# Last block of keys in a fused attention and expert kernel: three score products one place earlier, and the old maximum's weight sums added on GpSimd

## The chip, the core and the metric

The kernel runs on one core of a Trainium2 chip. A core has five engines that run side by side, each through its own queue in order: TensorE (PE: matrix products, with a separate queue for loading weights, PEld), VectorE (DVE), ScalarE (ACT), GpSimd (POOL) and SyncE (SP, which here issues all transfers). [...] The metric is the device time of one execution in microseconds (us); less is better.

## What is computed

One block of a network, in float32, on 128 rows `x` of width 512 and a context of 12544 rows: a cross-attention to the context (257 image rows, then text rows, each with its own softmax), a self-attention, and a routed mixture of experts. Only the cross-attention is touched:

```python
q = rms_norm(linear(x, q_w, q_b), norm_q_w)          # 16 heads of 32
k = rms_norm(linear(ctx_txt, k_w, k_b), norm_k_w)
v = linear(ctx_txt, v_w, v_b)
scores = einsum('bqhd,bkhd->bhqk', q, k) / sqrt(32)
probs  = softmax(scores)
txt_x  = einsum('bhqk,bkhd->bqhd', probs, v)
...
x = x + linear(txt_x + img_x, o_w, o_b)
```

## The kernel before, in words

**Tiling.** The text keys come in 24 blocks of 512 (the last has 511), block numbers 1 to 24; each block is cut into four tiles of 128 keys. Keys and values of a block are made by seven products of half-size blocks each (a Strassen scheme): `step(b, k, "k")` and `step(b, k, "v")` (line 1134) each issue one such product for block `b` and the VectorE or ScalarE instruction that takes it out of PSUM. The main loop (`for t in range(tile0[2], tile0[LAST])`) works on tile `t` and makes the next block's keys and values in between. What follows it is written out by hand for the last block, and this is where most of the change is.

**One tile.** For a tile, `weights(t)` (line 1249) first calls `scores(t)` (line 1162): 16 small products on PE into the one PSUM tile `sb` (four banks, one buffer). Then VectorE scales, subtracts the maximum and writes `p` (line 1258), and ScalarE takes the exponential in place (line 1266). `weigh` (line 1269) multiplies `p` by the values on PE (`av_new`). The softmax's denominator is gathered on GpSimd: `into_sums` (line 1427, instruction on line 1436) adds `p` into `ls`, and `half_into_sums` (line 1438, instruction on line 1440) does it in two halves of 1024 columns. `add_up` (line 1284) sums over the 128 keys of a tile on PE, into the PSUM bank `lpt`. `key_norms(b, js)` (line 1010) gives two tiles' norms: eight tiny PE products per tile pair (`ssq`), one or two VectorE instructions (`ms`), and GpSimd powers into `rinv`, which line 1258 reads. It needs `add_squares` (line 1126, two GpSimd additions on line 1130) to be done.

**Buffers.** `p` of most tiles lives in a pool of two buffers (`two`, tag `p`) that are handed out in turn; every third tile of the loop, and the first tile of the last block (`p_last`), has a buffer of its own. Call the last two tiles of block 23 Y and Z, and the four tiles of block 24 A, B, C and D (`t`, `t + 1`, `t + 2`, `t + 3`; D has 127 keys). Y and Z have the pool's two buffers, A has `p_last`, B gets Y's buffer, C gets Z's, D gets B's. A buffer is free when all readers of the tile before are done.

**Order.** Every instruction here goes through `pin` (line 838), so each engine's queue has the order of the program text. The queues of the stretch after the loop, before the change: PE: scores Z, keys step 7, norms A and B, scores A, weigh Y, weigh Z, keys step 4, values step 7, scores B, weigh A, values step 4, norms C and D, scores C, `lpt<-kept_l`, weigh B, add up B, scores D, weigh C, add up C, add up `ls`, add up D, weigh D. GpSimd: half sum Y, norms A and B, half sum Y, half sum Z, squares, half sum Z, norms C and D, sum A. After that come the reciprocals of `lpt`, the product with `w_o_w`, and the self-attention. `early_loads(0)` to `early_loads(2)` (line 1489) issue the next stage's weights into buffers as they come free.

**The old maximum.** The weights of the text tiles before tile `SWITCH` (the third of block 3) were taken against a first estimate of the maximum. From `SWITCH` on the kernel uses a better one; what was gathered before is multiplied by `shrink`. For the sums this is `kept_l`, made once at `SWITCH + 2` (line 1621, VectorE, from the PSUM bank `l_old`). In the kernel before it enters `lpt` by one product with the identity, on line 1684 in the last block.

Of the kernel before, what the change touches and what calls it, by code (L numbers as in the profile page):

```python
# [11 lines left out]
ALU = mybir.AluOpType  # L12
# [3 lines left out]
P = 128  # L16
# [4 lines left out]
XH, XHD = 16, 32  # L21
# [749 lines left out]
def fast_block(ctx: ExitStack, tc: tile.TileContext, a: dict, out: bass.AP, amiss: bass.AP):  # L771
    nc = tc.nc
# [11 lines left out]
    ident = const.tile([P, P], FP, tag="ident", name="ident")  # L784
# [53 lines left out]
    def pin(ins):  # L838

        return tc.keep_in_program_order(ins)  # L840
# [55 lines left out]
    with ExitStack() as xs:  # L896
# [113 lines left out]
        def key_norms(b, js):  # L1010

            ts = [blocks[b][3][j] for j in js]
            sp = bank(f"ssq_{b}_{js[0]}")
            for j, (o, m) in enumerate(ts):

                for r in range(0, m, XHD):
                    r1 = min(r + XHD, m)
                    pin(nc.tensor.matmul(  # L1018
                        sp[r:r1, j : j + 1],
                        lhsT=sq[b][:, 0, o + r : o + r1],  # L1020
                        rhs=ones[:, 0:1],
                        start=True,
                        stop=True,
                        skip_group_check=True,
                    ))
            ms = small.tile([P, 4], FP, tag="ms", name=f"ms_{b}_{js[0]}")
            t0 = tile0[b] + js[0]
            for j0, j1, m in row_groups(ts):
                pin(nc.vector.tensor_scalar(
                    ms[:m, j0:j1], sp[:m, j0:j1], 1.0 / D, 1e-6, ALU.mult, ALU.add  # L1030
                ))
                pin(inv_sqrt(rinv[:m, t0 + j0 : t0 + j1], ms[:m, j0:j1]))
# [101 lines left out]
        def step(b, k, kinds="kv"):  # L1134

            for kind in kinds:
                if k == 1:
                    if kind == "k":
                        kraw[b] = two.tile([P, NC, CHUNK], FP, tag="kraw", name=f"kraw_{b}")
                    else:  # L1140
                        vv[b] = two.tile([P, NC, D], FP, tag="v", name=f"v_{b}")
                    pin(nc.scalar.copy(piece(kind, "p1"), product(kind, b, 1, True)))  # L1142
                elif k == 2:
                    finish_quarter(kind, b, 0, 0, product(kind, b, 2, False), None)
                elif k == 6:
                    t = product(kind, b, 6, True)
                    pin(nc.vector.tensor_tensor(piece(kind, "z"), t, part_of[kind, "p1"], ALU.add))  # L1147
                elif k == 5:
                    t = product(kind, b, 5, True)
                    pin(nc.vector.tensor_tensor(piece(kind, "w"), t, part_of[kind, "z"], ALU.add))  # L1150
                elif k == 3:
                    finish_quarter(kind, b, 0, 1, product(kind, b, 3, False), part_of[kind, "z"])
                elif k == 7:
                    finish_quarter(kind, b, 1, 1, product(kind, b, 7, True), part_of[kind, "w"])
                elif k == 4:
                    finish_quarter(kind, b, 1, 0, product(kind, b, 4, False), part_of[kind, "z"])
                if kind == "k" and k in (3, 4):
                    squares(b, int(k == 4))
# [90 lines left out]
        def weights(t, s=None, p=None, parts=1):  # L1249

            b, part, o, m = tiles[t]
            if s is None:
                s = scores(t, "b")
            if p is None:
                p = two.tile([P, 4, CHUNK], FP, tag="p", name=f"p_{t}")
            n = 4 // parts
            for k in range(0, 4, n):
                pin(nc.vector.scalar_tensor_tensor(  # L1258
                    p[:m, k : k + n],
                    s[:m, k : k + n],  # L1260
                    rinv[:m, t : t + 1],
                    m_bc[part][:m, k : k + n],
                    ALU.mult,
                    ALU.subtract,
                ))
                pin(nc.scalar.activation(p[:m, k : k + n], p[:m, k : k + n], AF.Exp))  # L1266
            return p, s

        def weigh(t, p, first, last):

            b, part, o, m = tiles[t]
            for g in range(NC):
                for i in range(4):
                    hd = 4 * g + i
                    pin(nc.tensor.matmul(  # L1275
                        avp[part][i * XHD : (i + 1) * XHD, g, :],
                        lhsT=vv[b][:m, t - tile0[b], hd * XHD : (hd + 1) * XHD],
                        rhs=p[:m, i, g * P : (g + 1) * P],
                        start=(first and g == 0),
                        stop=(last and g == NC - 1),  # L1280
                        skip_group_check=True,
                    ))
# [64 lines left out]
        ps = [xc.tile([P, 4, CHUNK], FP, tag="ls", name="p_0")]  # L1347
# [61 lines left out]
        lp = bank("l_img")  # L1409
# [12 lines left out]
        SWITCH = tile0[RENEWED + 1] + 2  # L1422
        lsum = xc.tile([P, 4, CHUNK], FP, tag="ls", name="ls")
# [3 lines left out]
        def into_sums(t, p):  # L1427
            m = tiles[t][3]
            dst = [lsum[:m]] if t >= SWITCH else [h[:m] for h in ls_old]
            for k, d in enumerate(dst):  # L1430
                n = 4 // len(dst)
                src = p[:m, k * n : (k + 1) * n]
                if t in (t1, SWITCH):
                    pin(nc.gpsimd.tensor_copy(d, src))
                else:
                    pin(nc.gpsimd.tensor_tensor(d, d, src, op=ALU.add))  # L1436

        def half_into_sums(p, h):
            k = slice(2 * h, 2 * h + 2)
            pin(nc.gpsimd.tensor_tensor(lsum[:, k], lsum[:, k], p[:, k], op=ALU.add))  # L1440
# [100 lines left out]
        waiting = [pend]  # L1541
        AHEAD = range(NB - 8, NB - 2)
        for t in range(tile0[2], tile0[LAST]):
# [53 lines left out]
            if t == tile0[RENEWED + 1]:  # L1597
                m_new = xc.tile([P, 4, CHUNK], FP, tag="mx", name="mb_new")
                on_all(q_new, m_new, "new")
                pin(nc.vector.tensor_tensor(over, q_new, q_old, ALU.subtract))  # L1600
                less = small.tile([P, XH], FP, tag="less", name="less")
                pin(nc.scalar.activation(less, over, AF.Exp, scale=-1.0))
            elif t == tile0[RENEWED + 1] + 1:

                shrink = rowp.tile([P, D], FP, tag="h", name="shrink")
                on_heads(less, shrink, "less")
            elif t == SWITCH:
                av_old = avp["txt"].rearrange("p g q -> p (g q)")
                kept = {"av": row("kept_av", "kept_av")}
                pin(nc.vector.tensor_tensor(kept["av"], av_old, shrink, ALU.mult))  # L1610
                avp["txt"] = ps_o.tile([P, NC, P], FP, tag="o", name="av_new")
            elif t == SWITCH + 2:
                lp = bank("l_old")
                for i in range(4):
                    r = slice(i * XHD, (i + 1) * XHD)
                    pin(nc.tensor.matmul(
                        lp[r, :], lhsT=ones[:, :XHD], rhs=ls_old[i // 2][:, i % 2, :],
                        start=True, stop=True, skip_group_check=True,
                    ))
                kept["l"] = row("kept_l", "kept_l")  # L1620
                pin(nc.vector.tensor_tensor(kept["l"], lp, shrink, ALU.mult))
            if j == 2:
                make(b + 1, 3, "k")
            if b <= RENEWED:
# [38 lines left out]

        half_into_sums(unsummed[1], 0)
        step(b, 7, "k")
        key_norms(b, [0, 1])
        ps = [weights(t, p=xc.tile([P, 4, CHUNK], FP, tag="vw", name="p_last"))[0]]
        half_into_sums(unsummed[1], 1)
        for k_, p_ in waiting:
            weigh(k_, p_, False, False)  # L1670
        half_into_sums(p, 0)
        step(b, 4, "k")
        add_squares(b, 1)
        half_into_sums(p, 1)
        early_loads(0)
        step(b, 7, "v")
        ps.append(weights(t + 1)[0])
        weigh(t, ps[0], False, False)
        step(b, 4, "v")
        key_norms(b, [2, 3])  # L1680
        early_loads(1)
        ps.append(weights(t + 2)[0])
        lpt = bank("lpt")
        pin(nc.tensor.matmul(lpt, lhsT=ident, rhs=kept["l"], start=True, stop=False, skip_group_check=True))
        into_sums(t, ps[0])
        early_loads(2)
        weigh(t + 1, ps[1], False, False)
        add_up(lpt, ps[1], P, False, False)
        ps.append(weights(t + 3, parts=2)[0])
        weigh(t + 2, ps[2], False, False)  # L1690
        add_up(lpt, ps[2], P, False, False)
        add_up(lpt, lsum, P, False, False)
# [855 lines left out]
```

## Time and profile before

| what | value |
|---|---|
| device time, median of 3 runs | 1068.5 us (1067.93 to 1068.62) |
| device time of the profiled execution | 1066.76 us |
| its span (first to last instruction) | 1064.9 us, so 1.86 us lie around it |
| PE busy | 1047.9 us (98% of the span) |
| PEld, DVE, ACT, POOL busy | 829.6, 538.2, 360.1, 694.2 us |
| mean granted TensorE clock | 0.999 |
| stretch of the last block, 833 to 863 us: PE, PEld, DVE, ACT, POOL busy | 27.51, 19.35, 20.18, 12.52, 20.31 of 30 us |
| main loop, one block of four tiles | 33.5 us (from one block's first keys step to the next) |

How to read the views. In a timeline a line gives the start, the time from the first start to the last end, engine, source line, operation, output and inputs, shape and count; in brackets stands how long the engine had been idle, and whose end released it. Ends of PE products are modelled and overlap the next start, so for PE I take start to start. In the prediction all times are microseconds from the span's start.

### The profile page before, as it was taken

To read this page: it belongs to the slowest core of one execution; us is meant where nothing else is said; L and a number is where in the kernel's file an instruction comes from. 1 tells how busy PE (TensorE), PEld (TensorE's weight loads), DVE (VectorE), ACT (ScalarE), POOL (GpSimd) and SP (SyncE) were. 2 spreads that over 40 slices of the span, in tenths; PEclk is the share of its full clock that TensorE was granted. 3 is DMA by queue.
4 is the path that set the end of the run, shared out by engine and by line. 5 is a ranking of instruction groups with operands and counts; after the bars stand their busy time and mean duration, and the time that the engine had idled before them with its cause. 6 is when DMAs were issued, how large, how long until landed. Compare 5 with 4: busy or idle time off the path is not lost.

```text
span 1064.9 us, 24839 instructions
## 1 busy us (share of the span) xinstructions
PE 1047.9 (98%) x11076; PEld 829.6 (78%) x11076; DVE 538.2 (51%) x671; ACT 360.1 (34%) x438; POOL 694.2 (65%) x378
## 2 busy tenths in 40 slices
PE   9999999999999999999999999999999989999997
PEld 6768888888888888888888888888888769754332
DVE  2767764574445544455544555455444668442211
ACT  2353233333333333433334333343333424403111
POOL 2256888688888888888988889988999810000000
PEclk9999999999999999999999999999999999999999
DMA  9321021101111011110113301110010599629996
GB/s 298 108 81 37 6 81 50 41 2 41 41 41 41 2 41 41 42 39 3 42 45 116 101 14 41 41 41 15 27 41 2 172 353 389 224 72 412 415 413 241
DMA packets 43252, 113.25 MB, mean 106 GB/s; under 512 B 6720, under 2 KB 12032, under 8 KB 42112
## 3 DMA queue, kind: packets, MB, share of 16 engines
q1 hardware_dynamic: 43136, 111.57, 29.0%
q8 instruction: 89, 1.46, 0.6%
q14 instruction: 27, 0.22, 0.1%
HBM read 111.26 MB, written 0.29 MB: 105 GB/s over the span
## 4 chain that ended last, share of the span: by engine, by line
PE 94%; DVE 3%; ACT 1%; DMA 1%; POOL 1%; issue 0%; SPq 0%; DVEq 0%; ACTq 0%; POOLq 0%
PE kp L1085 28%; PE vp L1085 27%; PE sb L1169 10%; PE av_new L1275 7%; PE up L2135 5%; PE acc L2122 2%; PE qp L1794 1%; PE kp L1794 1%; PE yp L1952 1%; PE svp L1815 1%; PE y L2176 1%; PE vp L1237 1%; PE av_old L1275 1%; PE ssq L1018 1%; DVE p L1258 1%; DMA x<-in_x 1%
## 5 line engine op out<-in xcount | busy, mean ns | idle before, releaser
L1436 POOL TENSOR_TENSOR ls<-ls,p 128x2048 f32<-128x2048 f32 x79 | 359.7, 4553 | 31.0 <-ACT p L1266 31.0
L1266 ACT ACTIVATE p<-p 128x2048 f32<-128x2048 f32 (+1 forms) x95 | 179.9, 1893 | 437.3 <-DVE p L1258 425.7
L1258 DVE SCALAR_TENSOR_TENSOR p<-sb,rinv,mb_new 128x2048 f32<-128x2048 f32 (+1 forms) x86 | 199.9, 2325 | 108.8 <-PE sb L1169 107.1
L1130 POOL TENSOR_TENSOR sq<-sq 128x512 f32<-128x512 f32 x96 | 96.3, 1003 | 86.1 <-ACT sq L1124 82.3
L1169 PEld LDWEIGHTS sb<-qT_txt,kraw 32*128 32x128 f32 (+1 forms) x3040 | 93.4, 186 | 32.3 <-issue 30.7
L1169 PE MATMUL sb<-qT_txt,kraw 32*128 32x128 f32 (+1 forms) x3040 | 111.5, 283 | 0.4 <-DVE p L1258 0.4
L1085 PE MATMUL kp<-xs,w_k_w 128*128 128x256 f32 x384 | 95.4, 391 | 0.0
L1085 PE MATMUL kp<-ctx,w_k_w 128*128 128x256 f32 x384 | 93.2, 386 | 1.0 <-ACT kp L1142 1.0
L1085 PE MATMUL kp<-xs,kt 128*128 128x256 f32 x384 | 91.2, 380 | 0.1
L1085 PE MATMUL vp<-vt,xs 128*128 128x256 f32 x384 | 91.0, 380 | 0.0
L1085 PE MATMUL vp<-w_v_w,ctx 128*128 128x256 f32 x384 | 90.9, 380 | 0.0
L1085 PE MATMUL vp<-w_v_w,xs 128*128 128x256 f32 x384 | 90.8, 379 | 0.0
L1275 PE MATMUL av_new<-p,v 128*32 128x128 f32 (+1 forms) x2720 | 84.6, 274 | 0.5 <-ACT p L1266 0.5
L1085 PEld LDWEIGHTS kp<-xs,kt 128*128 128x128 f32 x384 | 72.5, 190 | 11.2 <-issue 0.9
L1085 PEld LDWEIGHTS vp<-vt,xs 128*128 128x128 f32 x384 | 72.7, 190 | 10.2 <-ACT kraw L1113 0.4
L1085 PEld LDWEIGHTS vp<-w_v_w,xs 128*128 128x128 f32 x384 | 72.8, 190 | 10.1
L1085 PEld LDWEIGHTS vp<-w_v_w,ctx 128*128 128x128 f32 x384 | 72.8, 190 | 10.0 <-issue 0.2
L1085 PEld LDWEIGHTS kp<-xs,w_k_w 128*128 128x128 f32 x384 | 69.2, 189 | 14.6 <-issue 4.8
L1085 PEld LDWEIGHTS kp<-ctx,w_k_w 128*128 128x128 f32 x384 | 70.8, 190 | 11.5 <-ACT kp L1142 1.4
L1275 PEld LDWEIGHTS av_new<-p,v 128*32 128x32 f32 (+1 forms) x2720 | 71.8, 110 | 7.1 <-ACT p L1266 1.4
L1147 DVE TENSOR_TENSOR kz<-kp,kp 128x512 f32<-128x512 f32 x24 | 16.6, 691 | 98.5 <-issue 93.9
L818 POOL TENSOR_TENSOR rs_x<-ve_x,neghalf 128x1 f32<-128x1 f32 x3 | 1.7, 552 | 95.5 <-DVE ve_x L826 95.5
(460 smaller groups left out, 1476.8 us busy)
## 6 DMA issues: line engine op xcount, KB each, us to landing
ctx<-in_ctxT SPq DMA_DIRECT2D x23, 1024.0 KB, 5.1
wo<-in_experts SPq DMA_DIRECT2D x18, 512.0 KB, 8.6
wo<-in_wo_codes SPq DMA_DIRECT2D x8, 512.0 KB, 6.3
wq<-in_experts SPq DMA_DIRECT2D x8, 512.0 KB, 9.8
wk<-in_experts SPq DMA_DIRECT2D x8, 512.0 KB, 9.5
wv<-in_experts SPq DMA_DIRECT2D x7, 512.0 KB, 10.0
q<-in_experts SPq DMA_DIRECT2D x7, 512.0 KB, 10.1
f<-in_experts SPq DMA_DIRECT2D x7, 512.0 KB, 10.0
```

The lines of the kernel that those rows point to most:

```text
L1018: pin(nc.tensor.matmul(sp[r:r1, j : j + 1], lhsT=sq[b][:, 0, o + r : o + r1], rhs=ones[:, 0:1], start=True, stop=True, skip_group_check=Tr ...
L1085: pin(nc.tensor.matmul(t[:, h, :], lhsT=lhs, rhs=rhs, start=(first and h == 0 and c == 0), stop=(h == 1 and c == 1), skip_group_check=True,))
L1130: pin(nc.gpsimd.tensor_tensor(sq[b][:, :w, ks], sq[b][:, :w, ks], sq[b][:, w : 2 * w, ks], op=ALU.add))
L1147: pin(nc.vector.tensor_tensor(piece(kind, "z"), t, part_of[kind, "p1"], ALU.add))
L1169: pin(nc.tensor.matmul(s[:m, i, g * P : (g + 1) * P], lhsT=kraw[b][rows, g, o : o + m], rhs=qT[part][rows, g, :], start=True, stop=True,))
L1258: pin(nc.vector.scalar_tensor_tensor(p[:m, k : k + n], s[:m, k : k + n], rinv[:m, t : t + 1], m_bc[part][:m, k : k + n], ALU.mult, ALU.sub ...
L1266: pin(nc.scalar.activation(p[:m, k : k + n], p[:m, k : k + n], AF.Exp))
L1275: pin(nc.tensor.matmul(avp[part][i * XHD : (i + 1) * XHD, g, :], lhsT=vv[b][:m, t - tile0[b], hd * XHD : (hd + 1) * XHD], rhs=p[:m, i, g * ...
L1436: pin(nc.gpsimd.tensor_tensor(d, d, src, op=ALU.add))
L1794: pin(nc.tensor.matmul(pp[:, k, :], lhsT=w[:, c, k * SHD : (k + 1) * SHD], rhs=hT2[:, c, :], start=(c == 0), stop=(c == NC - 1),))
L2122: pin(nc.tensor.matmul(acc, lhsT=lhsT, rhs=rhs, start=(n_acc == 0), stop=last))
L2135: pin(nc.tensor.matmul(up[r : r + m, :], lhsT=lhsT, rhs=w13_of((kind != "all", i), c), start=(c == 0), stop=(c == NC - 1), skip_group_chec ...
```

## The change

Two things are changed. In the main loop, `kept_l` is made 1/32 as large (`XHD` is 32), and GpSimd adds it to the running sums `ls`: for each of four groups of 32 partitions one addition of 32x512 elements, two at tile `SWITCH + 4` (block 4) and two at `SWITCH + 8` (block 5). The ones-product over `ls` at the end then contains it 32 times, so the identity product on line 1684 goes. In the last block the pieces are put in another order: weigh Y stands ahead of the norms of A and B; the scores of B, C and D each stand one product earlier (B ahead of values step 7, C ahead of values step 4, D ahead of the add up of B); the norms of C and D stand ahead of the second half sum of Z, and that half sum ahead of the weights of C.

```diff
                 kept["l"] = row("kept_l", "kept_l")
-                pin(nc.vector.tensor_tensor(kept["l"], lp, shrink, ALU.mult))
+                pin(nc.vector.scalar_tensor_tensor(kept["l"], lp, 1.0 / XHD, shrink, ALU.mult, ALU.mult))
+            elif t in (SWITCH + 4, SWITCH + 8):
+
+                for i in range(2 * (t == SWITCH + 8), 2 * (t == SWITCH + 8) + 2):
+                    r = slice(i * XHD, (i + 1) * XHD)
+                    pin(nc.gpsimd.tensor_tensor(lsum[r, i, :], lsum[r, i, :], kept["l"][r, :], op=ALU.add))
...
         half_into_sums(unsummed[1], 0)
         step(b, 7, "k")
+        weigh(*waiting[0], False, False)
         key_norms(b, [0, 1])
         ps = [weights(t, p=xc.tile([P, 4, CHUNK], FP, tag="vw", name="p_last"))[0]]
         half_into_sums(unsummed[1], 1)
-        for k_, p_ in waiting:
-            weigh(k_, p_, False, False)
+        weigh(*waiting[1], False, False)
         half_into_sums(p, 0)
         step(b, 4, "k")
         add_squares(b, 1)
-        half_into_sums(p, 1)
+        ps.append(weights(t + 1)[0])
         early_loads(0)
         step(b, 7, "v")
-        ps.append(weights(t + 1)[0])
         weigh(t, ps[0], False, False)
+        key_norms(b, [2, 3])
+        half_into_sums(p, 1)
+        ps.append(weights(t + 2)[0])
+        into_sums(t, ps[0])
         step(b, 4, "v")
-        key_norms(b, [2, 3])
         early_loads(1)
-        ps.append(weights(t + 2)[0])
+        weigh(t + 1, ps[1], False, False)
+        early_loads(2)
+        ps.append(weights(t + 3, parts=2)[0])
         lpt = bank("lpt")
-        pin(nc.tensor.matmul(lpt, lhsT=ident, rhs=kept["l"], start=True, stop=False, skip_group_check=True))
-        into_sums(t, ps[0])
-        early_loads(2)
-        weigh(t + 1, ps[1], False, False)
-        add_up(lpt, ps[1], P, False, False)
-        ps.append(weights(t + 3, parts=2)[0])
+        add_up(lpt, ps[1], P, True, False)
         weigh(t + 2, ps[2], False, False)
         add_up(lpt, ps[2], P, False, False)
         add_up(lpt, lsum, P, False, False)
```

## The prediction, as it was put on record

> **What bounds the kernel.** I read the page first, for the engine that is full and for the chain that ended last.
>
> ```profile
> PE 1047.9 (98%) x11076; PEld 829.6 (78%) x11076; DVE 538.2 (51%) x671; ACT 360.1 (34%) x438; POOL 694.2 (65%) x378
> ...
> PE 94%; DVE 3%; ACT 1%; DMA 1%; POOL 1%; issue 0%; SPq 0%; DVEq 0%; ACTq 0%; POOLq 0%
> ```
>
> PE is busy nearly always and carries 94% of the chain, so a change pays only by taking PE work or a PE wait away, and it costs wherever it makes PE wait. The share is an average, so I went to the stretch of the change, the timeline of PE in the last block:
>
> ```profile
> 849.35 1.17 PE L1169 MATMUL sb<-qT_txt,kraw 32*128 32x128 f32 x32
> 850.46 1.12 PE L1684 MATMUL lpt<-kept_l,ident 128*128 128x512 f32 x2
> 851.51 1.08 PE L1275 MATMUL av_new<-p,v 128*32 128x128 f32 x32
> 852.41 1.04 PE L1287 MATMUL lpt<-p,ones 128*32 128x512 f32 x8
> 853.38 1.17 PE L1169 MATMUL sb<-qT_txt,kraw 32*127 32x128 f32 x32
> 855.04 1.08 PE L1275 MATMUL av_new<-p,v 128*32 128x128 f32 x32 [0.49 <-ACT p L1266]
> ```
>
> These are scores C, the product that goes, weigh B, add up B, scores D and weigh C. From 835.83 (keys step 7) to here PE idles only twice: 0.38 us ahead of scores A (838.44) and 0.49 us ahead of weigh C. So there is little idle time to win. Next, GpSimd and VectorE in the same stretch:
>
> ```profile
> 845.64 2.09 POOL L1130 TENSOR_TENSOR sq<-sq 128x512 f32<-128x512 f32 x2 [0.68 <-ACT sq L1124]
> 847.69 2.38 POOL L1440 TENSOR_TENSOR ls<-ls,p 128x1024 f32<-128x1024 f32 x1
> 850.06 1.09 POOL L818 TENSOR_TENSOR rinv<-ms,neghalf 128x1 f32<-128x1 f32 x2
> 851.11 4.58 POOL L1436 TENSOR_TENSOR ls<-ls,p_last 128x2048 f32<-128x2048 f32 x1
> ```
>
> ```profile
> 846.42 2.35 DVE L1258 SCALAR_TENSOR_TENSOR p<-sb,rinv,mb_new 128x2048 f32<-128x2048 f32 x1 [0.54 <-PE sb L1169]
> ...
> 850.69 2.35 DVE L1258 SCALAR_TENSOR_TENSOR p<-sb,rinv,mb_new 128x2048 f32<-128x2048 f32 x1 [0.65 <-POOL rinv L818]
> 854.72 2.48 DVE L1258 SCALAR_TENSOR_TENSOR p<-sb,rinv,mb_new 127x1024 f32<-127x1024 f32 x2 [1.67 <-PE sb L1169]
> 859.43 1.77 DVE L1703 RECIPROCAL rl<-lpt 128x128 f32<-128x128 f32 x2 [2.24 <-PE lpt L1287]
> ```
>
> GpSimd is full from 845.64 to 855.7. C's weights (850.69) start when GpSimd has finished the first norm; that norm stands behind the second half sum of Z (847.69). D's weights (854.72) start right after scores D. The reciprocals at 859.43 open a VectorE tail that nothing shortens, and no PE wait on a DMA is shown after it.
>
> **Part 1, the additions in the loop.** Added: four GpSimd additions of 32x512. The trace has no 32-partition form on GpSimd. If time went by partitions, a quarter of a 128x512 row would be 0.3 us; if by columns, a whole one: 1.05 (att_img, line 1646) to 1.29 (xs). I take the upper, 2.1 to 2.6 us a pair. The cover:
>
> ```profile
> 201.17 2.08 POOL L1130 TENSOR_TENSOR sq<-sq 128x512 f32<-128x512 f32 x2 [3.95 <-ACT sq L1124]
> ...
> 226.32 4.58 POOL L1436 TENSOR_TENSOR ls<-ls,p 128x2048 f32<-128x2048 f32 x1 [1.11 <-ACT p L1266]
> 230.85 1.05 POOL L1646 TENSOR_TENSOR att_img<-att_img,vbs 128x512 f32<-128x512 f32 x1
> 234.24 2.08 POOL L1130 TENSOR_TENSOR sq<-sq 128x512 f32<-128x512 f32 x2 [2.34 <-ACT sq L1124]
> ```
>
> Block 4's pair falls into 3.95 us of GpSimd idling, block 5's into 2.34 us behind its sum; at worst 0.3 us sticks out. Queued behind it are the squares, a sum, two context sums and the norms at 243.39, which end at 244.09; the weights that read them start at 245.27, released by PE after 4.00 us of VectorE idling, so 1.2 us are spare and GpSimd idles 1.58 us again at 259.88. Cost: nothing. Without that cover it would be up to 5.2 us. Here a rule speaks against the change: the Trainium skill, "GPSIMD Engine Reference", section "Engine selection", wants two-input elementwise work on VectorE, since GpSimd is about twice as slow. Taken as a cost on the path, the four would be 4.2 to 5.2 us by the row above; by the idle times they lie in, 0. I go by the idle times. The new form of `kept_l` (0.68 us at 179.60, VectorE then idle) costs nothing either.
>
> **Part 2, the product taken out.** Line 1684 holds PE from 850.46 to 851.51: 1.05 us. It is worth that only if PE is what is late around it.
>
> **Part 3, the order in the last block, up to scores C.** Weigh Y fits ahead of the norms of A and B (a weigh takes 0.95; its exponential is done at 833.75), and then scores A start at 838.9 without their wait. But A's weights still start at 840.32: they wait for GpSimd's norm (839.57, 0.71 us), which stands behind a half sum that ends at 839.6 in both. Weigh Z waits for its exponential (840.33), keys step 4 starts at 841.35 instead of 841.43, scores B at 843.2 instead of 845.08, B's weights at 844.5 instead of 846.42. The squares come through keys step 4, VectorE, ScalarE (844.52) and GpSimd, unmoved, and end at 847.73. PE has then done values step 7 and weigh A by 847.1 and waits 0.7 us for them; scores C start at 848.1 instead of 849.35. Up to here 1.2 us are won on PE.
>
> **Part 4, the waits that follow.** In the new order GpSimd has the norms of C and D at about 848.4 (squares 847.73, `ssq` 0.30, `ms` 0.2 and handoffs of 0.05 to 0.1), 1.65 us sooner. But C's weights are written into Z's buffer, and Z's second half sum now stands behind the norms: 848.4 + 1.09 + 2.37 = 851.85. VectorE must wait for that reader. So C's weights start at 851.9, not 850.69: **+1.2 us**. Queued behind them on VectorE is values step 4's copy, which weigh C needs; it ends at 854.85, before C's exponential (856.2), and costs nothing. On PE values step 4 and weigh B end at 851.85, and scores D, which need `sb` empty, wait until C's weights end at 854.25: a new PE wait of 2.4 us. Scores D start at 854.3, not 853.38: **+0.9 us** (0.3 less than the 1.2, since PE came 0.34 us after C's weights before).
>
> D's weights go into B's buffer, and its last reader, add up B, now stands behind scores D on PE. Before they started 1.34 us after scores D (853.38 to 854.72). Now it is 1.11 us of scores, 1.04 of add up (852.41's row) and 0.14 of handoff, 2.29: **+0.95 us**. From D's weights to the reciprocals the way is the same, 4.71 us: two halves, their exponentials, add up D. PE is not late there: from 854.3 it has 1.11 + 0.97 + 0.95 + 0.87 + 0.86 = 4.76 us of work, to 859.06, and D's second exponential ends at 856.57 + 3.56 = 860.13. GpSimd's sum of A ends at 856.4, ahead of its add up.
>
> Sum: 0.9 + 0.95 = **+1.85 us** at the reciprocals (861.28). The 1.05 us of line 1684 and the 1.2 won earlier fall into PE's new wait and bring 0. As bounds: each of the two waits could be off by some 0.2 us in handoffs.
>
> **Part 5, transfers.** The order on SP is unchanged; the buffers of `early_loads` come free 0.1 us earlier (values of block 23), 1.3 earlier (squares), or 1.9 later (`ctx`, `vt`). The last are asked for at 852.38 and later, when SP is behind anyway, and their first readers are past 880. Cost 0. In the self-attention (870 to 925, PE busy 53.64 of 55) and the experts, PE shows no wait on a transfer, and the expert loads that start at 952.04 wait for VectorE's routing, which moves with the rest; so the 1.85 us go through to the end. The profiled execution's 1066.76 becomes 1068.6 (span 1066.75); on the median of the runs, 1068.5, it is 1070.35, or +0.17%. About 0.2% (2.1 us, lines at 1066.4 and 1070.6) is what a measurement of this kernel can tell from no change.
>
> **Rivals.** *PE stays full*: the buffers aren't what I take them for, scores C and D are in time, and PE saves 1.05 us and the 0.49 us wait: 1068.5 - 1.5 = 1067.0. For it speaks the full PE; against it, two buffers in turn and the place of their readers. *Only one of the two waits*: D's weights don't wait for add up B: +0.9, 1069.4. *The clock falls (slower)*: PE's new 2.4 us wait before scores D is its longest in the stretch. The Trainium skill, "TensorE: Matmul & The Clock Gate", section "What's actually happening", says an idle window of about 3.4 us halves the clock until about 3.4 us have been busy again. If it fell at 854.3, 3.4 us at half rate would do 1.7 us of work: +1.7 on top, 1072.05. It decides from the point where a whole window is idle. The rows: from 858 to 862 PE is busy 2.53 of 4 us and from 1056 to 1060 2.01 of 4, both at a granted 1.00; only 1060 to 1065, empty, shows 0.69. With weigh B at 851 and scores D at 854.3 no such window is empty. By the rule at its edge +1.7, by the rows 0; I take 0. My own case is near a line itself: 0.3 us more in handoffs puts it over 0.2%.
>
> **Chances.** Both waits as worked out 0.78, and by their spread of about 0.4 us 0.50 of that below 1070.6 and 0.28 above; one wait only 0.07; PE stays full 0.05, of which 0.02 gains over 0.2%; the clock falls 0.10. Faster 0.02, same 0.50 + 0.07 + 0.03 = 0.60, slower 0.38. The likeliest, 1070.35, is the forecast; its own spread is 1069.7 to 1071.2. To leave out no more than 2 in 10 the range goes down to 1068.9, past the one-wait case, and up to 1071.6.
>
> **What would show it.** Right: PE idle of about 2.4 us ahead of scores D, released by VectorE; C's weights released by GpSimd's line 1440, not by `rinv`; D's weights 2.3 us after scores D start; the reciprocals about 1.85 us later; GpSimd's loop without a new PE wait. Wrong: C's weights released at about 849.5, a reciprocal at or before 859.43, a granted clock below 1.00 between 854 and 866, or a block of the loop longer than 33.5 us.

## The result, and the profile after

| what | before | after |
|---|---|---|
| device time, median of 14 runs each | 1067.55 us (1066.35 to 1068.62) | 1070.08 us (1069.12 to 1071.29) |
| ratio to before | | 1.0025, 95% interval 1.0018 to 1.0032 |
| span of the profiled execution | 1064.9 us | 1067.5 us |
| mean granted TensorE clock | 0.999 | 0.999 |

The kernel became slower by 2.5 us (interval 1.9 to 3.4). The forecast was 1070.35; it stood on a median of three runs for the kernel before, 1068.5, which 14 runs put at 1067.55. So the level was 0.95 us too high and the forecast step, +1.85, 0.7 us too small. The two errors go against each other; that the forecast lies only 0.3 us from the measured 1070.08 is in part luck.

The page's line of engines and its line of chain shares, after:

```profile
PE 1047.1 (98%) x11074; PEld 828.0 (78%) x11074; DVE 538.2 (50%) x671; ACT 360.2 (34%) x438; POOL 699.3 (66%) x382
...
PE 90%; DVE 3%; POOL 2%; ACT 1%; DMA 1%; issue 1%; SPq 0%; DVEq 0%; ACTq 0%; POOLq 0%
```

PE has two products less and 0.8 us less to do, GpSimd four instructions and 5.1 us more. The chain now spends 2% in GpSimd (1% before) and 90% in PE (94% before): PE has become a little less the engine that is late, which is the sign to look for. Where it waits stands in the timeline of PE in the last block:

```profile
848.20 0.30 PE L1018 MATMUL ssq<-ones,sq 128*32 128x1 f32 x16 [0.38 <-POOL sq L1130]
848.43 1.17 PE L1169 MATMUL sb<-qT_txt,kraw 32*128 32x128 f32 x32
...
854.67 1.17 PE L1169 MATMUL sb<-qT_txt,kraw 32*127 32x128 f32 x32 [2.13 <-DVE p L1258]
855.77 1.06 PE L1287 MATMUL lpt<-p,ones 128*32 128x512 f32 x8
```

Scores C start early, at 848.43. Scores D then wait 2.13 us for VectorE, where the kernel before had none. The next two views show why, GpSimd first and then VectorE, after:

```profile
846.03 2.11 POOL L1130 TENSOR_TENSOR sq<-sq 128x512 f32<-128x512 f32 x2 [0.69 <-ACT sq L1124]
848.81 1.08 POOL L818 TENSOR_TENSOR rinv<-ms,neghalf 128x1 f32<-128x1 f32 x2 [0.67 <-DVE ms L1029]
849.86 2.37 POOL L1440 TENSOR_TENSOR ls<-ls,p 128x1024 f32<-128x1024 f32 x1
```

```profile
852.27 2.35 DVE L1258 SCALAR_TENSOR_TENSOR p<-sb,rinv,mb_new 128x2048 f32<-128x2048 f32 x1 [3.47 <-POOL ls L1440]
856.97 2.48 DVE L1258 SCALAR_TENSOR_TENSOR p<-sb,rinv,mb_new 127x1024 f32<-127x1024 f32 x2 [1.76 <-PE lpt L1287]
861.69 1.77 DVE L1707 RECIPROCAL rl<-lpt 128x128 f32<-128x128 f32 x2 [2.24 <-PE lpt L1287]
```

The norms come first (848.81), the half sum of Z after them (849.86 to 852.23), and C's weights start 0.04 us after its end: line 1440 is now named as their releaser, where it was `rinv`. D's weights are released by the add up of B (`lpt`, line 1287), where they were released by scores D itself.

To see what the last block alone lost, I count from a common point, the start of scores Z (834.73 before, 835.11 after), to the reciprocals: 24.70 us before, 26.58 after, so **+1.88**. From the reciprocals to the end of the span it is 205.47 before and 205.81 after (205.4 to 205.8 in all kernels of this study), so the last block's loss goes through to the end.

The rest of the 2.6 us between the two spans, from the same two traces: the start is 0.78 us shorter (the input `x` lands at 9.40 instead of 10.17); the stretch from 150 to 168 us is 0.98 longer, where the code is the same in both (last section); block 5 of the loop is 0.19 longer; the tail 0.34. Only block 5 among these has to do with the change. GpSimd there, after, and then the weight load on PE that follows it, before and after:

```profile
226.52 4.57 POOL L1436 TENSOR_TENSOR ls<-ls,p 128x2048 f32<-128x2048 f32 x1 [1.05 <-ACT p L1266]
231.17 2.61 POOL L1626 TENSOR_TENSOR ls<-ls,kept_l 32x512 f32<-32x512 f32 x2
233.85 1.04 POOL L1651 TENSOR_TENSOR att_img<-att_img,vbs 128x512 f32<-128x512 f32 x1
234.85 2.07 POOL L1130 TENSOR_TENSOR sq<-sq 128x512 f32<-128x512 f32 x2
```

```profile
236.59 0.22 PEld L1018 LDWEIGHTS ssq<-ones,sq 128*32 128x32 f32 x16
...
236.97 0.22 PEld L1018 LDWEIGHTS ssq<-ones,sq 128*32 128x32 f32 x16 [0.31 <-POOL sq L1130]
```

GpSimd runs from 226.52 to 236.92 with no gap over 0.1 us, and the norm product waits for the squares. Before, the squares ended at 236.32 and that product started at 236.59: 0.27 us lay between, of which the handoff takes some 0.06 (236.92 to 236.98, after). The pair takes 2.61 us, so the squares slip by 0.39 us against the scores on PE (their end is 1.23 us after the scores' start instead of 0.84), and PE waits for the 0.18 that are not covered.

### The profile page after: what moved, and what is told of

The parts are those of the page before. It is cut to its first block, busy times and chain, and to the rows that moved or that the text cites. A ratio compares the mean times of both kernels' runs of the same rounds, so it can differ in the third digit from the quotient of the medians.

```text
span 1067.5 us, 24843 instructions
## 1 busy us (share of the span) xinstructions
PE 1047.1 (98%) x11074; PEld 828.0 (78%) x11074; DVE 538.2 (50%) x671; ACT 360.2 (34%) x438; POOL 699.3 (66%) x382
## 4 chain that ended last, share of the span: by engine, by line
PE 90%; DVE 3%; POOL 2%; ACT 1%; DMA 1%; issue 1%; SPq 0%; DVEq 0%; ACTq 0%; POOLq 0%
PE kp L1085 27%; PE vp L1085 25%; PE sb L1169 9%; PE av_new L1275 7%; PE up L2139 5%; PE acc L2126 2%; PE qp L1798 1%; PE kp L1798 1%; PE yp L1956 1%; PE svp L1819 1%; PE y L2180 1%; DVE p L1258 1%; PE vp L1237 1%; POOL sq L1130 1%; PE ssq L1018 1%
```

## The experiments

**The theories.** Mine: the loss is two buffer waits of nearly equal size in the last block, C's weights behind the half sum of Z, and D's weights behind the add up of B; the loop's additions cost up to 0.2 us beside them. A rival, the loop: the additions in the loop carry the loss (GpSimd has 5.1 us more to do). Another, a disturbance: what is lost comes from the clock or the transfers that the new waits disturb, so that undoing one wait brings much more or much less than that wait. Every kernel was timed in five rounds beside the kernel before on the same chip. "Last block" below is scores Z to reciprocals in the kernel's trace, against 24.70 us before.

**e1, the additions alone.** From the kernel before, only the loop's additions (with `kept_l` made 1/32 as large) and the removal of the identity product; the last block keeps its old order.

```diff
...
+            elif t in (SWITCH + 4, SWITCH + 8):
+
+                for i in range(2 * (t == SWITCH + 8), 2 * (t == SWITCH + 8) + 2):
+                    r = slice(i * XHD, (i + 1) * XHD)
+                    pin(nc.gpsimd.tensor_tensor(lsum[r, i, :], lsum[r, i, :], kept["l"][r, :], op=ALU.add))
...
-        pin(nc.tensor.matmul(lpt, lhsT=ident, rhs=kept["l"], start=True, stop=False, skip_group_check=True))
```

> The loop's part alone: kept_l is added to ls on GpSimd in blocks 4 and 5 and the identity product is gone, but the last block has the old order. Two-waits theory (the loss is C's weights behind the second half sum of Z, and D's weights behind add up B): block 5 is 0.2 us later, as in the profile after; in the last block weigh B starts at its exponential, 0.75 us earlier, and scores D then wait for C's weights and start 0.3 us earlier. Net -0.1 us, not to be told from before; no PE wait over 0.5 us in the last block. Rival (the additions in the loop are the cost, in the profile or in the runs): +2 us or more.

Measured: 1067.10 beside 1067.11, ratio 0.9997 (0.9988 to 1.0005). The last block takes 24.42 us, 0.28 less; in block 5 the time from the scores to the norm product that waits is 1.27 us instead of 1.11. PE's timeline, e1:

```profile
853.62 1.17 PE L1169 MATMUL sb<-qT_txt,kraw 32*127 32x128 f32 x32 [0.39 <-DVE p L1258]
```

The 1.05 us of the product are gone, but scores D then wait 0.39 us for C's weights to empty `sb`, and start only 0.28 sooner. With 0.16 lost in block 5 the sum is -0.1, as measured within the interval. The rival, the loop as the carrier of the loss, is out: it asked for +2 us or more.

**e2, the order alone.** The new order, with the loop as before and the identity product kept, after weigh B.

```diff
-            elif t in (SWITCH + 4, SWITCH + 8):
-
-                for i in range(2 * (t == SWITCH + 8), 2 * (t == SWITCH + 8) + 2):
...
         weigh(t + 1, ps[1], False, False)
+        lpt = bank("lpt")
+        pin(nc.tensor.matmul(lpt, lhsT=ident, rhs=kept["l"], start=True, stop=False, skip_group_check=True))
         early_loads(2)
         ps.append(weights(t + 3, parts=2)[0])
-        lpt = bank("lpt")
-        add_up(lpt, ps[1], P, True, False)
+        add_up(lpt, ps[1], P, False, False)
```

> The new order of the last block alone: the loop is as before, and the identity product is kept, placed after weigh B, ahead of scores D. Two-waits theory: the 1.05 us product lies in PE's new wait of 2.1 us and costs nothing; scores D +0.9, D's weights +1.9, so +1.9 us against before. Rival (loop additions): 0 to +0.2 us. Rival (PE's amount of work decides): +2.6 or more, 1.05 above the changed kernel without its loop part.

Measured: 1069.31 beside 1067.11, ratio 1.0019 (1.0011 to 1.0026). The last block takes 26.57 us, +1.87, the same as with the product removed. PE's timeline, e2:

```profile
855.05 1.17 PE L1169 MATMUL sb<-qT_txt,kraw 32*127 32x128 f32 x32 [1.07 <-DVE p L1258]
```

PE's wait is 1.07 instead of 2.13 us: the product fits into the wait whole, and the reciprocals don't move. The order alone makes the loss, and in it the product is worth nothing.

**e3, the first wait undone.** The half sum of Z ahead of the norms of C and D again.

```diff
         weigh(t, ps[0], False, False)
-        key_norms(b, [2, 3])
         half_into_sums(p, 1)
+        key_norms(b, [2, 3])
         ps.append(weights(t + 2)[0])
```

> The changed kernel with the second half sum of Z put back ahead of the norms of C and D. Two-waits theory: C's weights wait for the norm as before (850.7 in the times of before), scores D start at 853.1, D's weights still wait for add up B: +0.66 in the last block and 0.2 in the loop, +0.85 us against before. Rival (D's wait for add up B doesn't count, since PE or ScalarE is late anyway): about 0. Rival (loop): +2.

Measured: 1068.46 beside 1067.11, ratio 1.0015 (1.0008 to 1.0021); last block 25.35 us, +0.65. VectorE's timeline, e3:

```profile
850.44 2.35 DVE L1258 SCALAR_TENSOR_TENSOR p<-sb,rinv,mb_new 128x2048 f32<-128x2048 f32 x1 [2.21 <-POOL rinv L818]
855.18 2.48 DVE L1258 SCALAR_TENSOR_TENSOR p<-sb,rinv,mb_new 127x1024 f32<-127x1024 f32 x2 [1.79 <-PE lpt L1287]
```

C's weights are released by `rinv` again, as before the change, and the wait on the add up is still there. 1.88 - 0.65 = 1.23 us go.

**e4, the second wait undone.** The add up of B ahead of scores D again.

```diff
-        ps.append(weights(t + 3, parts=2)[0])
         lpt = bank("lpt")
         add_up(lpt, ps[1], P, True, False)
+        ps.append(weights(t + 3, parts=2)[0])
```

> The changed kernel with add up B put back ahead of scores D. Two-waits theory: add up B falls into PE's wait; C's weights end at 854.25 as in the changed kernel, scores D at 854.3, D's weights 1.34 us later: +0.9 in the last block and 0.2 in the loop, +1.1 us against before. Rival (the half sum's wait doesn't count): about 0.2. Rival (loop): +2.

Measured: 1068.45 beside 1067.11, ratio 1.0013 (1.0007 to 1.0020); last block 25.58 us, +0.88. VectorE's timeline, e4:

```profile
856.05 2.48 DVE L1258 SCALAR_TENSOR_TENSOR p<-sb,rinv,mb_new 127x1024 f32<-127x1024 f32 x2 [0.76 <-PE sb L1169]
```

D's weights follow scores D once more, and 1.88 - 0.88 = 1.00 us go. The add up itself costs PE nothing there, since PE was waiting.

**e5, both undone.** The two edits above together; everything else of the change stays.

> The changed kernel with both put back: the second half sum of Z ahead of the norms, and add up B ahead of scores D; the earlier scores of B and C, the norms ahead of values step 4 and the loop's additions stay. Two-waits theory: C's weights at 850.7 as before, scores D at 853.1 (before 853.38), -0.3 in the last block and +0.2 in the loop: -0.1 us, not to be told from before. Rival (loop additions, or any other part of the new order): +1 us or more.

Measured: 1067.27 beside 1067.38, ratio 0.9998 (0.9989 to 1.0006); last block 24.34 us, -0.36. VectorE's timeline, e5, C's weights and then D's:

```profile
852.52 2.35 DVE L1258 SCALAR_TENSOR_TENSOR p<-sb,rinv,mb_new 128x2048 f32<-128x2048 f32 x1 [2.21 <-POOL rinv L818]
...
856.26 2.48 DVE L1258 SCALAR_TENSOR_TENSOR p<-sb,rinv,mb_new 127x1024 f32<-127x1024 f32 x2 [0.79 <-PE sb L1169]
```

Both have the releasers that they had before the change. Together the two edits take 2.24 us away, 1.23 and 1.00 one by one: the waits are independent and add up, and with both gone nothing of the last block's loss is left. A disturbance of the clock or the transfers would have needed a remainder or an interaction, and the last block of these traces shows none.

**e6, another buffer for C.** The new order is kept whole, but C's weights go into a tile of their own (in the pool `two`, under the tag `ctx` of the context rows, where one is free by then), so they wait for no reader of Z; D then takes the pool's next buffer, Z's, whose readers are done, so that the add up of B holds nothing up either.

```diff
         ps.append(weights(t + 1)[0])
+        p_c = two.tile([P, 4, CHUNK], FP, tag="ctx", name="p_c")
         early_loads(0)
...
-        ps.append(weights(t + 2)[0])
+        ps.append(weights(t + 2, p=p_c)[0])
```

> The changed kernel, its order kept, but C's weights go into a free buffer (that of block 23's context, which the next stage takes over later); D then gets Z's buffer. Neither wait is left. Two-waits theory: C's weights start at 849.4 after scores C, scores D at 852.05 (PE, no wait), D's weights at 853.4, 1.3 earlier than before; then GpSimd's sum of A, which ends at 856.4, is late for its add up, and the reciprocals come at 858.45: -1.0 in the last block, +0.2 in the loop, -0.8 us against before. Rival (the new order itself costs, whatever the buffers): +1 us or more. Rival (loop): +1.

Measured: 1066.67 beside 1067.38, ratio 0.9995 (0.9988 to 1.0001); last block 23.83 us, -0.87. PE's timeline and then VectorE's, e6:

```profile
852.48 1.17 PE L1169 MATMUL sb<-qT_txt,kraw 32*127 32x128 f32 x32
...
856.97 1.07 PE L1287 MATMUL lpt<-ls,ones 128*32 128x512 f32 x8 [0.60 <-POOL ls L1436]
```

```profile
849.73 2.35 DVE L1258 SCALAR_TENSOR_TENSOR p_c<-sb,rinv,mb_new 128x2048 f32<-128x2048 f32 x1 [0.93 <-DMA sc<-in_wv_scales]
...
853.81 2.48 DVE L1258 SCALAR_TENSOR_TENSOR p<-sb,rinv,mb_new 127x1024 f32<-127x1024 f32 x2 [1.13 <-PE sb L1169]
```

The early start of C pays now: its weights begin 1.29 us after scores C (848.44). The view names a transfer as their releaser, but in e7, where the code here is the same, it names scores C, with 1.30 us; so the transfer hardly held them. Scores D begin without a wait and D's weights 1.33 us after them. What is late next is GpSimd's sum of A, for which PE waits 0.60 us.

**e7, the same with the additions spread.** e6 with one 32x512 addition per block, over four blocks, instead of two blocks with two.

```diff
-            elif t in (SWITCH + 4, SWITCH + 8):
-
-                for i in range(2 * (t == SWITCH + 8), 2 * (t == SWITCH + 8) + 2):
-                    r = slice(i * XHD, (i + 1) * XHD)
-                    pin(nc.gpsimd.tensor_tensor(lsum[r, i, :], lsum[r, i, :], kept["l"][r, :], op=ALU.add))
+            elif t in (SWITCH + 4, SWITCH + 8, SWITCH + 12, SWITCH + 16):
+                i = (t - SWITCH) // 4 - 1
+                r = slice(i * XHD, (i + 1) * XHD)
+                pin(nc.gpsimd.tensor_tensor(lsum[r, i, :], lsum[r, i, :], kept["l"][r, :], op=ALU.add))
```

> As with C's own buffer, and GpSimd's four additions of kept_l spread over blocks 4 to 7, one each. Two-waits theory: an addition of 1.3 us fits into each block's GpSimd idling (2.34 us and more), so PE's norms in block 5 don't wait: -1.0 us against before, 0.2 below the version with two additions a block; the time can hardly show the 0.2, the profile's start of the squares in block 5 can. Rival (loop additions are the cost): no difference to two a block.

Measured: 1066.48 beside 1067.38, ratio 0.9988 (0.9981 to 0.9995), the only kernel here whose whole interval lies below the kernel before, by 0.1%; last block 23.82 us, -0.88. GpSimd in block 5, e7:

```profile
232.47 1.27 POOL L1625 TENSOR_TENSOR ls<-ls,kept_l 32x512 f32<-32x512 f32 x1
235.75 2.07 POOL L1130 TENSOR_TENSOR sq<-sq 128x512 f32<-128x512 f32 x2 [0.89 <-ACT sq L1124]
```

GpSimd idles 0.89 us ahead of the squares, and from the scores to the norm product it is 1.10 us, as before the change (1.11). The loop's cost is gone. The step from e6 to e7 in whole runs (0.9995 to 0.9988) is inside the two intervals; the trace of block 5 shows it.

## Why the prediction was right, and where it was not

The time lies in the range and the mechanism was the forecast one; the size of the step and its class were not; the term that was mis-sized is the cost of the loop's additions (part 1), and 0.5 us more stay open. All times in this section are differences of starts, each counted from the start of scores Z in its own trace, so that what moved earlier in the kernel drops out.

**Part 3, up to scores C: right.** Scores C came 1.30 us sooner (14.62 to 13.32); some 1.2 were forecast. That start is worth nothing as long as C's buffer isn't free, and e6 shows what it is worth when it is: the last block falls below the kernel before by 0.87.

**Part 4, the first wait: right.** C's weights +1.20 (forecast +1.2), scores D +0.91 (+0.9). PE's wait is 2.13 us by the view, and 2.3 from start to start, as the prediction counts it; forecast were 2.4. e3 removes it, with 1.23 us. That is 0.3 more than the 0.9 the sum has for it. In e3 scores D start 0.35 sooner than in the kernel before (18.30 us after scores Z, against 18.65), because the identity product no longer stands ahead of them; e1 shows much the same, 0.28.

**Part 4, the second wait: right.** D's weights start 2.30 us after scores D (forecast 2.29; 1.34 before): +0.96. e4 removes it, with 1.00. The reciprocals are at +1.88 (forecast +1.85).

**Part 2, the identity product: right.** Worth 0 beside PE's new wait (e2 against after: 26.57 and 26.58), and in the old order 0.28 of its 1.05 us (e1).

**Part 5, transfers and the tail: right within the scatter.** 205.47 and 205.81 from the reciprocals to the end; the kernels of this study lie between 205.4 and 205.8, and no wait on a transfer was added.

**Part 1, "Cost: nothing": mis-sized.** The upper price per pair was the right one (2.61 us), and "at worst 0.3 us sticks out" was nearly so (0.39). But the working followed the delay to the reader of the norms at 245.27 only, with 1.2 us to spare. The squares have a reader before that, the norm product on PE, and it has 0.27 us to spare, less the handoff. It costs 0.16 to 0.18 in the kernels with two additions in a block, and nothing in e7 with one, nor in e2 with none. In the weighing of the row against the rule on two-input work on GpSimd, the idle times were the nearer guide: 4.2 to 5.2 us by the rule taken on the path, 0 by the idle times, 0.17 measured.

**The chances.** The class within 0.2% had 0.60; the measured ratio is 1.0025, in the class that had 0.38. The prediction said that 0.3 us more in handoffs would put it over. The handoffs did not bring it: 0.03 in the last block. Block 5 brought 0.17. The two parts make 2.05 us, which is itself close to the line (2.1), and 2.53 were measured, with an interval of 1.9 to 3.4 that holds both. The 0.5 between them was not settled. e2, with the last block's +1.87 alone, measured +2.0 (1.2 to 2.8); e3 measured +1.6 (0.9 to 2.2) where its trace gives 0.82, and e4 +1.4 (0.7 to 2.1) where its trace gives 1.05. Two things on record could make part of such an excess, and neither is shown to. One is the transfer of the last section, which costs PE 0.5 to 1.0 us in some executions. The other is the granted clock: of the 14 executions after, seven have a mean of 0.999 and a median time of 1069.29 us, the other seven 0.995 to 0.997 and 1070.58. Beside e1 to e7, 21 of 109 executions of the kernel before have 0.996 or 0.997; for the 14 executions of it above no clock is on record.

**The rivals.** *PE stays full* fell by the buffers, and came about in part in e6 and e7, where these were changed (-0.7 and -0.9 us in whole runs instead of its -1.5, since PE now waits 0.6 us for GpSimd's sum of A). *Only one of the two waits* is what e3 and e4 look like (+0.65 and +0.88), not the change. *The clock falls* did not come in the trace after. Its stretches of 4 us, with busy time and count of PE, PEld, DVE, ACT and POOL, then the granted clock:

```profile
850.00:854.00 4.00, 2.54 (x40) 1.81 (x38) 1.73 (x1) 0.00 (x0) 3.92 (x2) 1.00 0.91 259
854.00:858.00 4.00, 3.33 (x80) 2.22 (x84) 2.24 (x3) 1.91 (x1) 2.87 (x1) 1.00 1.01 396
```

PE is busy 2.54 of 4 us around its wait of 2.13, and the clock stays at 1.00 in it and after it. But that execution has a mean clock of 0.999. None of the seven with a lower one left a trace, so where the clock fell in these stays open. The one trace with a mean of 0.996 is that of e5, and there it fell at the start of the kernel:

```profile
6.00:8.00 2.00, 0.52 (x2) 0.46 (x3) 0.00 (x0) 0.36 (x1) 0.00 (x0) 0.90 1.02 333
8.00:10.00 2.00, 2.00 (x6) 1.61 (x5) 0.25 (x1) 0.92 (x1) 0.00 (x0) 0.50 1.03 422
```

PE had waited 1.92 us there for a transfer (to 7.48), and the clock was at one half from 7.6 to 11.1 us. So a wait of 1.92 us came before a fall in e5, and the wait of 2.13 us in after did not: the length of the wait alone does not decide, and the prediction's condition, that a whole window of about 3.4 us is idle, is not what e5 shows.

## What to carry to other kernels

A step that is moved ahead writes a buffer: before it is moved, name the last reader of what that buffer held, and see where this reader now stands in its own engine's queue, since a score product one place sooner is worth nothing when the sum or the add up that frees its buffer has been put behind it. When a move leaves one short wait on another engine, giving that one tile a buffer of its own can turn the same order from a loss (+1.88 us in the last block) into a gain (-0.87). Work put into an engine's idle time costs nothing only if the first reader of what comes next in that queue has as much to spare; look at the nearest reader (0.27 us here), not at the one that the engine shows as waiting later (1.2 us).

## What was not expected of the hardware

**A transfer that reads what the last one wrote.** At 157 us the kernel writes `max_less` by a transfer and reads it back in another layout as `shrink`; SP issues the read when the write has landed (1.3 us after its issue before, 3.5 after). The queue of SP, before, and then after:

```profile
157.23 0.32 SPq L1212 DMA_DIRECT2D max_less<-qmt_less  x1
...
158.59 1.90 SPq L1224 DMA_DIRECT2D shrink<-max_less  x4
```

```profile
156.46 0.32 SPq L1212 DMA_DIRECT2D max_less<-qmt_less  x1
...
159.97 1.71 SPq L1224 DMA_DIRECT2D shrink<-max_less  x4
```

From issue to issue 1.36 us in the one and 3.51 in the other. The instructions up to there are the same, and the kernels of the study fall into two groups: 1.36 in before, e3 and e5, 3.06 to 3.51 in after, e1, e2, e4, e6 and e7. The loop's additions are in kernels of both groups (e1 long, e3 and e5 short), and so is the new order (e2 long, e3 short), so neither part of the change goes with the long time. In every one of the nine traces one of two such writes is slow: where `max_less` lands after 1.3 us, the write of `max_new` some 10 us earlier lands after 3.2 to 3.6, and where `max_less` takes 3.0 to 3.5, `max_new` takes 1.4. So it seems to belong to the single execution, as far as one trace of each can tell, and not to the change; where `max_less` is the slow one, PE is 0.5 to 1.0 us later. Whoever compares two single traces would take this for an effect of the change.

**An addition over 32 partitions on GpSimd** takes 1.26 to 1.28 us for 32x512 elements, no less than over 128 partitions: 1.27 for the 128x512 addition of the squares, 1.27 to 1.30 for `xs`, 1.04 for `att_img`. (A pair of squares takes 2.07 us because its second addition has only 128x256 elements, 0.73 us.) The time goes by the columns (2.37 us for 128x1024, 4.55 for 128x2048); cutting the partitions to a quarter saves nothing.
